# A two-stream GRU's last eight steps: r and z in one product, another order of turns, other places for late shares

## The chip, the cores and the metric

The kernel runs on one core of a Trainium2 chip. The metric is device time in microseconds (us) of one execution; lower is better. Each kernel is executed several times, and one further execution is recorded by the hardware profiler.

## The reference

Two layers work on x (64 sequences, 128 steps, 512 features, float32), with cond (64 x 512).

```python
x = x + L0(x, cond)      # gated linear recurrence, computed with cumulative sums
x = x + L1(cond, x)      # a conditioned GRU

# L1: 128 steps, one after the other, on h (64 x 512), h0 = 0
z  = sigmoid(x_t @ W_z + h @ U_z + vz)
r  = sigmoid(x_t @ W_r + h @ U_r + vr)
hh = tanh(x_t @ W + (r * h) @ U + vh)
h  = (1 - z) * h + z * hh
```

vz, vr and vh are products of cond with C_z, C_r, C, plus biases. The output is x after both residual sums, all 128 steps.

## The kernel before, in words

The first layer is done by feature chunks and takes the first third of the time. The rest of the span is the GRU, whose 128 steps depend on each other.

The 64 sequences are split into two streams of 32 (class Stream, s = 0 and 1). While one stream's step waits for its sigmoids and products, TensorE works for the other. A stream's state h is kept in a packed form: 128 partitions, of which each quarter of 32 holds the 32 sequences for 128 of the 512 features. hT is the same state transposed within 32 x 32 blocks, which makes it fit to be loaded as weights; U is the moving operand. matmuls (L459) takes a product apart in 4 parts of the contraction (k) and 4 quarters of the output (q); in float32 each of these 16 matmuls shows as two weight loads and two matmuls in the trace.

What does not depend on h, x_t @ W plus the v terms, is called a share. The shares of eight steps (a group) are computed together, as seven outer products of a fast (Strassen-Winograd) scheme with seven inner ones each (class Outer, products at L602, adds at L704 and L719 to L724). They are stored to DRAM (L732), read back for each stream and step as four transfers of 48 KB (load_share, L854 to L865), and copied into the PSUM tile g by ScalarE (put_share), where the products with h are then added up. Even steps are loaded into the tile xz (two buffers, one for each stream in effect), odd steps into the stream's whole_v. A load must therefore wait for the copy of the step two before it.

halves (L893) writes one step of one stream in two halves. In the ordinary order (steps up to 120) they are:

- first half: one product of 256 columns for r and z (of_state, L917); sigmoid r (L918); in two halves of the columns, r*h (L922) and its transposition (L923), both on DVE; sigmoid z (L927); on POOL 1-z (L933) and (1-z)*h (L934), both in the place of r. In the gaps go products of the next group (place), reads of finished ones, and the outputs of the step before (deferred).
- second half: the candidate product (L954, printed under L464), tanh (L957), the copy of the next share (L871), z*hh (L969), the new h (L970), its transposition (L974), and on POOL the sum with x for the output (L985).

From step 121 on (APART) no products of shares are left, and the halves become three parts: r's product of 128 columns; then z's product into a PSUM tile of its own (gz); then the candidate. A round, one step of both streams, takes the parts in the order 0 0 1 0 1 1. There ScalarE computes 1-z as sigmoid(-z) (L930), DVE computes (1-z)*h (L931) and the output's sum (L978), and the new h is made in two halves of the columns (L969 to L972), so that its first half can be loaded while the second is made. Outputs of the last eight steps are gathered in o_last and stored by L1028: four steps at once after step 123, two after steps 125 and 127.

Each engine runs its own queue in order. pin() keeps an instruction behind the one before it on its engine, as the program is written. The SP queue (SyncE) issues nearly all transfers; those that are not pinned may be put ahead by the scheduler at build time, by what it takes to be ready first.

Of the kernel before, what the change touches and what calls it, by code (L numbers as in the profile page):

```python
# [9 lines left out]
F32 = mybir.dt.float32  # L10
# [9 lines left out]
def kernel(  # L20
# [58 lines left out]
    def pin(instruction):  # L79
        return tc.keep_in_program_order(instruction)  # L80
# [751 lines left out]
    def direct(st, t):  # L832

        return t < 8

    class Stream:
        def __init__(self, s):
            self.s = s
            self.whole_v = vs[s]
            self.batches = slice(s * SB, (s + 1) * SB)  # L840
            self.h = self.hT = None

            self.g = psum.tile([P, 3, P], F32, tag="p0", name=f"g{s}")

            self.rz = fs[s][:, : 4 * P].rearrange("p (n e) -> p n e", e=P)
            self.home = self.g
            self.early = {}
            self.shares = {}  # L850
            self.outputs = {}
            self.gz = None

        def load_share(self, t):  # L854

            assert all((t, q) in stored for q in range(Q)), (self.s, t)
            if t % 2 == 0:
                share = work.tile([P, 3 * P], F32, tag="xz", bufs=2, name=f"xz{self.s}_{t}")
            else:
                share = self.whole_v.rearrange("p g e -> p (g e)")  # L860
            self.shares[t] = share
            n = t % TW * B + self.s * SB
            rows = shares_d[t // TW % len(shares_d)][n : n + SB]
            for q in range(Q):
                nc.sync.dma_start(share[q * SB : (q + 1) * SB], rows[:, q])  # L865

        def put_share(self, t):

            share = self.shares.pop(t).rearrange("p (g e) -> p g e", e=P)
            if t < APART:  # L870
                pin(nc.scalar.copy(self.g, share))  # L871
                return
            if self.gz is None:
                self.gz = psum.tile([P, 1, P], F32, tag="p2", name=f"gz{self.s}")
            pin(nc.scalar.copy(self.g[:, ::2], share[:, ::2]))
            pin(nc.scalar.copy(self.gz, share[:, 1:2]))

        def put_v(self):

# [13 lines left out]
        def halves(self, t, filler=None, between=None, targets=lambda: (0, 0), busy=False, reads=(4, 0)):  # L893
# [2 lines left out]

            r, z, rh, rhT = (self.rz[:, n] for n in range(4))
            h_, hT_, g = self.h, self.hT, self.g
            apart = t >= APART

            def of_state(gates, xT_, g=g):
                matmuls(
                    g if g is self.gz else g[:, gates],
                    lambda k: xT_[:, k * SB : (k + 1) * SB],
                    [w_s[:, k, gates] for k in range(K)],
                    start=False,
                )
# [6 lines left out]
            if t == 0:  # L914
                pin(nc.scalar.activation(z, g[:, 1], AF.Sigmoid))
            else:
                of_state(slice(0, 2 - apart), hT_)  # L917
                pin(nc.scalar.activation(r, g[:, 0], AF.Sigmoid))  # L918

                for n in range(2 - apart):  # L920
                    e = slice(0, P) if apart else slice(n * HC * SB, (n + 1) * HC * SB)
                    pin(nc.vector.tensor_tensor(rh[:, e], r[:, e], h_[:, e], ALU.mult))  # L922
                    pin(nc.vector.transpose(rhT[:, e], rh[:, e]))  # L923
                if apart:
                    yield
                    of_state(slice(1, 2), hT_, self.gz)
                pin(nc.scalar.activation(z, self.gz[:, 0] if apart else g[:, 1], AF.Sigmoid))  # L927

                if apart:
                    pin(nc.scalar.activation(r, self.gz[:, 0], AF.Sigmoid, scale=-1.0))  # L930
                    pin(nc.vector.tensor_tensor(r, r, h_, ALU.mult))  # L931
                else:
                    pin(nc.gpsimd.tensor_scalar(r, z, -1.0, 1.0, ALU.mult, ALU.add))  # L933
                    pin(nc.gpsimd.tensor_tensor(r, r, h_, ALU.mult))  # L934
            while shared_to_copy:
                shared_to_copy[0]()
            add(1)
# [24 lines left out]
            elif t == S - 1:  # L962
# [4 lines left out]
            for n in range(1 + apart) if t else ():  # L967
                e = slice(n * HC * SB, (n + 1) * HC * SB) if apart else slice(0, P)
                pin(nc.vector.tensor_tensor(hh[:, e], hh[:, e], z[:, e], ALU.mult))  # L969
                pin(nc.vector.tensor_tensor(h[:, e], hh[:, e], r[:, e], ALU.add))  # L970
                if apart:
                    pin(nc.vector.transpose(hT[:, e], h[:, e]))  # L972
            if not apart or t == 0:
                pin(nc.vector.transpose(hT, h))  # L974
            self.h, self.hT = h, hT

            def output():
                pin(nc.vector.tensor_tensor(o, o, h, ALU.add))  # L978
                self.store(t)

            if apart:
                deferred.append(output)
                return
            pin(
                nc.gpsimd.tensor_tensor(  # L985
# [9 lines left out]
                self.store(t)  # L995

            deferred.append(output)
            if APART <= t + AHEAD < S:
# [5 lines left out]
            if t + 2 < S and not direct(self, t + 2) and all((t + 2, q) in stored for q in range(Q)):  # L1004
                self.load_share(t + 2)

        def output(self, t):
            if t // 4 not in self.outputs:
# [10 lines left out]
        def store(self, t):  # L1019
            if t == S - 1 or t == S - 3:  # L1020
                ts = slice(t - 1, t + 1)
            elif t % 4 == 3:
                ts = slice(t - 3, t + 1)
            else:
                return
            for q in range(Q):
                queue = nc.scalar if t == S - 1 and self.s and q % 2 else nc.sync
                queue.dma_start(  # L1028
                    out_parts[q, self.batches, ts],
                    self.outputs[t // 4][q * SB : (q + 1) * SB, ts.start % 4 : (ts.stop - 1) % 4 + 1],  # L1030
                )

    APART, AHEAD = 121, 10
    last_outputs = []
    deferred = []
    pending = []
# [222 lines left out]
    def take(n):  # L1261
        st, ts = streams[order[n][0]], order[n][1]
        at = FIRST + n
        twice = n + 1 < len(order) and order[n + 1][0] == st.s
        busy = at < GOALS[3][0]
        todo = pending[:]
        pending.clear()
        together = min(order[n][1], order[min(n + 1, len(order) - 1)][1]) >= APART
        yield from st.halves(
            ts,  # L1270
            filler=lambda: [f() for f in todo],
            targets=lambda: (
                0 if together else goal(at + 1) - 1 - 2 * twice if busy else state["placed"] + 2,
                goal(at + 1 + st.s * together) + 2 * twice,
            ),
            busy=busy,
            between=lambda: late(n),
            reads=(0, 2) if together else (2, 2) if twice else (4, 1 * busy),
        )
        if ts + 1 in st.early:  # L1280
            st.g = st.early.pop(ts + 1)
        elif direct(st, ts + 1):
            st.put_v()
            f = lambda: st.x_products(ts + 1)
            f() if twice else pending.append(f)
        if n > 0 and order[n - 1][0] == st.s:
            return

        tick = 2 * order[n - st.s][1] + st.s if n else FIRST
        if tick in (FIRST, FIRST + 1):  # L1290
            sums_to_take.extend(sum_tasks(1)[tick - FIRST])
            take_sums(4)
        for w in range(2, NX):
            n_ = tick - 16 * w
            if w == 2 and n_ == -23:
                load_window(w)
                ahead_of[w] = gathers(w)
            elif w > 2 and -30 <= n_ < -26:
                load_window(w, qs=range(n_ + 30, n_ + 31))
                ahead_of[w] = gathers(w)  # L1300
            elif (-25 if w > 2 else -22) <= n_ < -21:
                gather(ahead_of[w], 2 if w > 2 else 4)
            elif w == 2 and n_ in (-20, -19):
                gather(ahead_of[w], 2)
            if n_ == (-21 if w > 2 else -19):
                sums_to_take.extend(sum_tasks(w))

    n = 0
    while n < len(order):
        together = n + 1 < len(order) and order[n][0] == 0 and order[n][1] >= APART  # L1310
        steps = [take(n + i) for i in range(1 + together)]

        for i in (0, 0, 1, 0, 1, 1) if together else (0, 0):
            next(steps[i], None)
        n += len(steps)
    while deferred:
# [36 lines left out]
```

## Time and profile before

| | us |
|---|---|
| median of 3 runs | 1877.04 |
| lowest and highest | 1876.59, 1879.87 |
| the profiled execution | 1878.12 |
| its span, first to last instruction | 1876.3 |
| TensorE busy | 1864.2 (99%) |
| VectorE (DVE) busy | 1504.9 (80%) |
| ScalarE (ACT) busy | 722.6 (39%) |
| GpSimd (POOL) busy | 865.1 (46%) |

The granted TensorE clock was 0.999 of full speed. All stamps below count from the start of the span. In rows of the timeline the columns are: start, duration, engine, line of the kernel, operation, output and inputs by the program's names ("fi" is the tile that holds r, z, r*h and its transposition; "h" the one that holds hh, the new h and hT), shapes, the number of instructions merged, and in brackets the idle time of the engine before it with what ended it. "issue" is idle time in which the profile shows nothing to wait for. In the windows table a row gives a stretch, its length, TensorE's busy time with the number of matmuls, the granted clock, the share of the DMA engines that was busy, and GB/s. The page's third part gives, for a DMA queue, packets, megabytes and share.

Step 120's first product starts at 1822.14; the first products of the rounds 121 to 127 start at 1830.06, 1835.31, 1841.71, 1847.39, 1853.79, 1859.52 and 1865.76.

### The profile page before, as it was taken

What the parts mean: (1) busy time and instruction counts of PE and PEld (TensorE: products, weight loads), DVE (VectorE), ACT (ScalarE), POOL (GpSimd) and SP (SyncE); (2) the same over time, 40 slices, a digit from 0 to 9 for tenths busy, and PEclk for the clock granted to TensorE, in tenths of its full rate; (3) what the DMA queues carried; (4) which work ended last, traced back from release to release, by engine and by line L of the source; (5) the groups of instructions that cost most, each with busy time, mean ns of one, the idle gap of its engine ahead of it and who ended that gap; (6) DMA issues with size and microseconds to landing.
All of it is one profiled execution on the core that took longest, in us unless ns stands there. A gap on an engine that the chain in (4) does not pass through costs nothing.

```text
span 1876.3 us, 62311 instructions
## 1 busy us (share of the span) xinstructions
PE 1864.2 (99%) x24793; PEld 1054.2 (56%) x24793; DVE 1504.9 (80%) x3438; ACT 722.6 (39%) x1888; POOL 865.1 (46%) x1544
## 2 busy tenths in 40 slices
PE   9999999999999999999999999999999999999998
PEld 5444444444444445566666666666666666666567
DVE  5899999999999976777777777777777777777786
ACT  3232223222232233344444444444444444444434
POOL 1233232333333344546556556466565565565650
PEclk9999999999999999999999999999999999999999
DMA  7765433444333241334334344344343343443343
GB/s 181 176 124 119 82 70 73 88 82 83 73 76 65 49 86 29 101 90 142 112 101 142 94 115 133 104 124 126 96 137 109 99 141 101 114 130 96 111 111 78
DMA packets 366754, 195.38 MB, mean 104 GB/s; under 512 B 225332, under 2 KB 352064, under 8 KB 366464
## 3 DMA queue, kind: packets, MB, share of 16 engines
q1 hardware_dynamic: 366280, 191.33, 40.9%
q8 instruction: 195, 3.19, 0.7%
q14 instruction: 95, 0.78, 0.1%
q10 hardware_dynamic: 184, 0.07, 0.0%
HBM read 78.63 MB, written 81.13 MB: 85 GB/s over the span
## 4 chain that ended last, share of the span: by engine, by line
PE 98%; DVE 1%; issue 0%; DMA 0%; ACT 0%; SPq 0%; DVEq 0%; ACTq 0%
PE g L464 36%; PE p L232 35%; PE r L602 14%; PE r12a L602 4%; PE shared L602 4%; PE r12b L602 4%; PE gz L464 1%; PE tp L190 0%; PE pv L464 0%; DMA x<-in_x_dram 0%; DVE W L704 0%; PE g_first L464 0%; DVE fi L923 0%; DVE fi L922 0%; DVE r L339 0%
## 5 line engine op out<-in xcount | busy, mean ns | idle before, releaser
L232 PE MATMUL p<-xT,W 128*128 128x512 f32 (+1 forms) x1560 | 661.9, 586 | 0.0
L232 PEld LDWEIGHTS p<-xT,W 128*128 128x128 f32 x1560 | 293.5, 190 | 361.6 <-issue 359.1
L464 PE MATMUL g<-w_s,h 128*32 128x256 f32 (+1 forms) x8128 | 481.0, 373 | 2.3 <-issue 1.6
L464 PEld LDWEIGHTS g<-w_s,h 128*32 128x32 f32 x8128 | 301.4, 110 | 179.4 <-issue 83.2
L464 PEld LDWEIGHTS g<-w_s,fi 128*32 128x32 f32 x8128 | 222.7, 109 | 113.9 <-issue 55.4
L464 PE MATMUL g<-w_s,fi 128*32 128x128 f32 x8128 | 276.3, 273 | 2.7 <-DVE fi L922 1.3
L922 DVE TENSOR_TENSOR fi<-fi,h 128x64 f32<-128x64 f32 (+1 forms) x494 | 112.3, 227 | 179.3 <-ACT fi L918 178.5
L985 POOL TENSOR_TENSOR h<-h,x 128x128 f32<-128x128 f32 x242 | 121.3, 501 | 232.4 <-DVE h L974 206.8
L314 POOL COPY first<-condT 128x4 f32<-128x4 f32 x64 | 12.6, 196 | 461.8 <-DVE h L386 432.8
L918 ACT ACTIVATE fi<-g 128x128 f32<-128x128 f32 x254 | 70.6, 278 | 327.7 <-PE g L464 308.9
L933 POOL TENSOR_SCALAR fi<-fi 128x128 f32<-128x128 f32 x240 | 72.6, 302 | 236.6 <-DVE fi L922 226.5
L704 DVE TENSOR_TENSOR W<-r,W 128x384 f32<-128x384 f32 x315 | 169.2, 539 | 7.4
L310 ACT ACTIVATE fi<-fi 128x512 f32<-128x512 f32 x64 | 40.4, 631 | 340.6 <-DVE fi L351 340.6
L957 ACT ACTIVATE h<-g 128x128 f32<-128x128 f32 x255 | 70.9, 278 | 236.2 <-PE g L464 236.2
L923 DVE STREAM_TRANSPOSE fi<-fi 128x64 f32<-128x64 f32 (+1 forms) x494 | 122.2, 247 | 22.8 <-PE r12a L602 0.5
L969 DVE TENSOR_TENSOR h<-h,fi 128x128 f32<-128x128 f32 (+1 forms) x264 | 94.9, 359 | 43.8 <-ACT h L957 43.1
L253 POOL TENSOR_TENSOR x<-xT,h 128x512 f32<-128x512 f32 x63 | 122.6, 1946 | 4.9
L934 POOL TENSOR_TENSOR fi<-fi,h 128x128 f32<-128x128 f32 x240 | 110.8, 462 | 20.0
L970 DVE TENSOR_TENSOR h<-h,fi 128x128 f32<-128x128 f32 (+1 forms) x264 | 97.7, 370 | 27.2 <-POOL held L810 0.9
L810 POOL TENSOR_TENSOR held<-held 128x128 f32<-128x128 f32 x240 | 113.7, 488 | 3.1
L602 PE MATMUL r<-w_inner,held 128*32 128x384 f32 x1080 | 114.6, 486 | 0.0
L339 DVE RECIPROCAL r<-r 128x256 f32<-128x256 f32 x60 | 104.2, 1737 | 0.0
(158 smaller groups left out, 2721.5 us busy)
## 6 DMA issues: line engine op xcount, KB each, us to landing
shares<-W SPq DMA_DIRECT2D x240, 192.0 KB, 2.1
xz<-shares SPq DMA_DIRECT2D x480, 48.0 KB, 1.9
whole_v<-shares SPq DMA_DIRECT2D x480, 48.0 KB, 2.0
x2d<-x SPq DMA_DIRECT2D x63, 256.0 KB, 4.2
words<-held SPq DMA_DIRECT2D x240, 64.0 KB, 2.1
out_dram<-o SPq DMA_DIRECT2D x240, 64.0 KB, 1.8
xw_None<-x2d SPq DMA_DIRECT2D x56, 256.0 KB, 3.4
w_rows<-in_L_cond_W_f_dram SPq DMA_DIRECT2D x4, 256.0 KB, 5.7
```

The costliest lines, as they stand in the source:

```text
L232: nc.tensor.matmul(p[:, tokens], lhsT=W0[:, c, n, k, :], rhs=xT[g][:, k, tokens], start=(k == 0), stop=(k == K - 1),)
L253: nc.gpsimd.tensor_tensor(x2.rearrange("p (t b) -> p t b", b=GB)[:, ts], xT[g][:, c, :].rearrange(f"{layout(g)} -> p t b", b=GB)[:, ts], b ...
L339: pin(nc.vector.reciprocal(r, r))
L464: nc.tensor.matmul(p[q * SB : (q + 1) * SB], lhsT=lhsT(k), rhs=part(wk, q), start=(start and k == 0), stop=(stop and k == len(w) - 1), ski ...
L602: nc.tensor.matmul(self.bank(bank)[q * SB : (q + 1) * SB], lhsT=a[:, q * SB : (q + 1) * SB], rhs=w_, start=start, stop=True, skip_group_ch ...
L704: pin(nc.vector.tensor_tensor(dst, r, other, ALU.add))
L810: pin(nc.gpsimd.tensor_tensor(*a))
L922: pin(nc.vector.tensor_tensor(rh[:, e], r[:, e], h_[:, e], ALU.mult))
L923: pin(nc.vector.transpose(rhT[:, e], rh[:, e]))
L934: pin(nc.gpsimd.tensor_tensor(r, r, h_, ALU.mult))
L970: pin(nc.vector.tensor_tensor(h[:, e], hh[:, e], r[:, e], ALU.add))
L985: nc.gpsimd.tensor_tensor(hh.rearrange("p (k b) -> p k b", b=SB), hT.rearrange("p (k b) -> p k b", b=SB), x_of(self, t), ALU.add,)
```

## The change

- The separate order now begins at step 120 (TURNS) instead of 121, and has two halves again: one product of 256 columns for r and z, and the candidate. A round's order is 0 1 0 1. The tile gz is gone; the share is copied to PSUM in one instruction.
- In these steps r*h is made and transposed in two halves; ScalarE still computes sigmoid(-z), into the place of r; (1-z)*h and the output's sum are on POOL.
- Shares of steps 123 to 127 (LATE) get places of their own, in v_x and held, whose contents are no longer needed. In the second half of step 120 a stream loads its shares up to step 125, in that of step 121 the rest. Share loads and output stores of steps from 120 on are pinned on their queue.

```diff
         def load_share(self, t):
-            if t % 2 == 0:
+            if t >= LATE:
+                share = late_shares(self.s, t)
+            elif t % 2 == 0:
                 share = work.tile([P, 3 * P], F32, tag="xz", bufs=2, name=f"xz{self.s}_{t}")
...
-                nc.sync.dma_start(share[q * SB : (q + 1) * SB], rows[:, q])
+                in_order(t, nc.sync.dma_start(share[q * SB : (q + 1) * SB], rows[:, q]))
...
         def put_share(self, t):
-            if t < APART:
-                pin(nc.scalar.copy(self.g, share))
-                return
...
-            pin(nc.scalar.copy(self.g[:, ::2], share[:, ::2]))
-            pin(nc.scalar.copy(self.gz, share[:, 1:2]))
+            pin(nc.scalar.copy(self.g, share))
...
-                of_state(slice(0, 2 - apart), hT_)
+                of_state(slice(0, 2), hT_)
                 pin(nc.scalar.activation(r, g[:, 0], AF.Sigmoid))
-                for n in range(2 - apart):
-                    e = slice(0, P) if apart else slice(n * HC * SB, (n + 1) * HC * SB)
+                for n in range(2):
+                    e = slice(n * HC * SB, (n + 1) * HC * SB)
                     pin(nc.vector.tensor_tensor(rh[:, e], r[:, e], h_[:, e], ALU.mult))
                     pin(nc.vector.transpose(rhT[:, e], rh[:, e]))
-                if apart:
-                    yield
-                    of_state(slice(1, 2), hT_, self.gz)
-                pin(nc.scalar.activation(z, self.gz[:, 0] if apart else g[:, 1], AF.Sigmoid))
-                if apart:
-                    pin(nc.scalar.activation(r, self.gz[:, 0], AF.Sigmoid, scale=-1.0))
-                    pin(nc.vector.tensor_tensor(r, r, h_, ALU.mult))
+                pin(nc.scalar.activation(z, g[:, 1], AF.Sigmoid))
+                if turns:
+                    pin(nc.scalar.activation(r, g[:, 1], AF.Sigmoid, scale=-1.0))
                 else:
                     pin(nc.gpsimd.tensor_scalar(r, z, -1.0, 1.0, ALU.mult, ALU.add))
-                    pin(nc.gpsimd.tensor_tensor(r, r, h_, ALU.mult))
+                pin(nc.gpsimd.tensor_tensor(r, r, h_, ALU.mult))
...
             def output():
-                pin(nc.vector.tensor_tensor(o, o, h, ALU.add))
+                pin(nc.gpsimd.tensor_tensor(o, o, h, ALU.add))
                 self.store(t)
+            def load_next(last):
+                for n in range(t + 2, min(last, S - 1) + 1):
+                    if n not in self.shares and not direct(self, n) and all((n, q) in stored for q in range(Q)):
+                        self.load_share(n)
-            if apart:
+            if turns:
                 deferred.append(output)
+                load_next(max(t + 2, S - 1 if t > TURNS else LATE + 2))
                 return
...
-    APART, AHEAD = 121, 10
+    TURNS, AHEAD, LATE = 120, 10, 123
+    def in_order(t, transfer):
+        return pin(transfer) if t >= TURNS else transfer
+    def late_shares(s, t):
+        n = 2 * (t - LATE) + s
+        if n < Q:
+            return v_x[:, n].rearrange("p g e -> p (g e)")
+        return held.rearrange("p n e -> p (n e)")[:, (n - Q) * 3 * P : (n - Q + 1) * 3 * P]
...
-        for i in (0, 0, 1, 0, 1, 1) if together else (0, 0):
+        for i in (0, 1, 0, 1) if together else (0, 0):
             next(steps[i], None)
```

More of the change, by code (lines that the diff above doesn't have):

```diff
@@ L851, in __init__ @@
             self.outputs = {}
-            self.gz = None
         def load_share(self, t):
             assert all((t, q) in stored for q in range(Q)), (self.s, t)
-            if t % 2 == 0:
+            if t >= LATE:
+                share = late_shares(self.s, t)
+            elif t % 2 == 0:
                 share = work.tile([P, 3 * P], F32, tag="xz", bufs=2, name=f"xz{self.s}_{t}")
@@ L864, in load_share @@
             for q in range(Q):
-                nc.sync.dma_start(share[q * SB : (q + 1) * SB], rows[:, q])
+                in_order(t, nc.sync.dma_start(share[q * SB : (q + 1) * SB], rows[:, q]))
         def put_share(self, t):
             share = self.shares.pop(t).rearrange("p (g e) -> p g e", e=P)
-            if t < APART:
-                pin(nc.scalar.copy(self.g, share))
-                return
-            if self.gz is None:
-                self.gz = psum.tile([P, 1, P], F32, tag="p2", name=f"gz{self.s}")
-            pin(nc.scalar.copy(self.g[:, ::2], share[:, ::2]))
-            pin(nc.scalar.copy(self.gz, share[:, 1:2]))
+            pin(nc.scalar.copy(self.g, share))
         def put_v(self):
@@ L898, in halves, with of_state @@
             h_, hT_, g = self.h, self.hT, self.g
-            apart = t >= APART
-            def of_state(gates, xT_, g=g):
+            turns = t >= TURNS
+            def of_state(gates, xT_):
                 matmuls(
-                    g if g is self.gz else g[:, gates],
+                    g[:, gates],
                     lambda k: xT_[:, k * SB : (k + 1) * SB],
@@ L966, in halves @@
                 return
-            for n in range(1 + apart) if t else ():
-                e = slice(n * HC * SB, (n + 1) * HC * SB) if apart else slice(0, P)
+            for n in range(1 + turns) if t else ():
+                e = slice(n * HC * SB, (n + 1) * HC * SB) if turns else slice(0, P)
                 pin(nc.vector.tensor_tensor(hh[:, e], hh[:, e], z[:, e], ALU.mult))
                 pin(nc.vector.tensor_tensor(h[:, e], hh[:, e], r[:, e], ALU.add))
-                if apart:
+                if turns:
                     pin(nc.vector.transpose(hT[:, e], h[:, e]))
-            if not apart or t == 0:
+            if not turns:
                 pin(nc.vector.transpose(hT, h))
@@ L977, in output @@
             def output():
-                pin(nc.vector.tensor_tensor(o, o, h, ALU.add))
+                pin(nc.gpsimd.tensor_tensor(o, o, h, ALU.add))
                 self.store(t)
-            if apart:
+            def load_next(last):
+                for n in range(t + 2, min(last, S - 1) + 1):
+                    if n not in self.shares and not direct(self, n) and all((n, q) in stored for q in range(Q)):
+                        self.load_share(n)
+            if turns:
                 deferred.append(output)
+                load_next(max(t + 2, S - 1 if t > TURNS else LATE + 2))
                 return
@@ L997, in halves @@
             deferred.append(output)
-            if APART <= t + AHEAD < S:
+            if TURNS <= t + AHEAD < S:
                 pin(nc.gpsimd.tensor_copy(ident.rearrange("p (k b) -> p k b", b=SB), x_of(self, t + AHEAD)))
@@ L1003, in halves @@
             read(reads[1])
-            if t + 2 < S and not direct(self, t + 2) and all((t + 2, q) in stored for q in range(Q)):
-                self.load_share(t + 2)
+            load_next(t + 2)
         def output(self, t):
@@ L1027, in store @@
                 queue = nc.scalar if t == S - 1 and self.s and q % 2 else nc.sync
-                queue.dma_start(
-                    out_parts[q, self.batches, ts],
-                    self.outputs[t // 4][q * SB : (q + 1) * SB, ts.start % 4 : (ts.stop - 1) % 4 + 1],
-                )
-    APART, AHEAD = 121, 10
+                in_order(
+                    t,
+                    queue.dma_start(
+                        out_parts[q, self.batches, ts],
+                        self.outputs[t // 4][q * SB : (q + 1) * SB, ts.start % 4 : (ts.stop - 1) % 4 + 1],
+                    ),
+                )
+    TURNS, AHEAD, LATE = 120, 10, 123
[6 more added lines that the diff above has]
+        return held.rearrange("p n e -> p (n e)")[:, (n - Q) * 3 * P : (n - Q + 1) * 3 * P]
     last_outputs = []
@@ L1267, in take @@
         pending.clear()
-        together = min(order[n][1], order[min(n + 1, len(order) - 1)][1]) >= APART
+        together = min(order[n][1], order[min(n + 1, len(order) - 1)][1]) >= TURNS
         yield from st.halves(
@@ L1273, in take @@
                 0 if together else goal(at + 1) - 1 - 2 * twice if busy else state["placed"] + 2,
-                goal(at + 1 + st.s * together) + 2 * twice,
+                goal(at + 1) + 2 * twice,
             ),
@@ L1277, in take @@
             between=lambda: late(n),
-            reads=(0, 2) if together else (2, 2) if twice else (4, 1 * busy),
+            reads=(2, 0) if together else (2, 2) if twice else (4, 1 * busy),
         )
@@ L1309 @@
     while n < len(order):
-        together = n + 1 < len(order) and order[n][0] == 0 and order[n][1] >= APART
+        together = n + 1 < len(order) and order[n][0] == 0 and order[n][1] >= TURNS
         steps = [take(n + i) for i in range(1 + together)]
-        for i in (0, 0, 1, 0, 1, 1) if together else (0, 0):
+        for i in (0, 1, 0, 1) if together else (0, 0):
             next(steps[i], None)
```

## The prediction

> **What bounds the kernel now.** I read the page first, then the last steps in the windows table, then single rows of the timeline.
>
> ```profile
> q8 instruction: 195, 3.19, 0.7%
> ...
> PE 98%; DVE 1%; issue 0%; DMA 0%; ACT 0%; SPq 0%; DVEq 0%; ACTq 0%
> ```
>
> The chain that ended last is TensorE for 98% of the span, so up to step 119, where the diff changes no arithmetic, nothing can be gained. All that matters lies in the last 54 us (1822.14, the first r,z product of step 120, to 1876.3). There each pair of steps (one of each stream: a round) has 3.49 us of r,z products (2 x 32 instructions of 256 columns, 1.73 each, or the same work in 128 columns) and 1.75 us of candidate products (2 x 0.873): 5.24 us. The windows run from one round's first product to the next, for steps 120, 122 and 123:
>
> ```profile
> 1822.14:1830.06 7.92, 5.65 (x136) 1.00 0.54 143
> ...
> 1835.31:1841.71 6.40, 5.74 (x197) 1.00 0.36 83
> 1841.71:1847.39 5.68, 5.55 (x203) 1.00 0.31 74
> ```
>
> The six rounds of steps 121 to 126 run from 1830.06 to 1865.76: 5.95 us each, 0.71 above the products. Step 120, still in the ordinary order, takes 7.92. Part of the 0.71 is not a wait for data:
>
> ```profile
> 1836.33 0.75 PE L464 MATMUL g<-w_s,h 128*32 128x128 f32 x19 [0.42 <-issue]
> ...
> 1840.27 0.75 PE L464 MATMUL gz<-w_s,h 128*32 128x128 f32 x20 [0.24 <-issue]
> ```
>
> TensorE stops with nothing to wait for, and between the two stops lie 127 recorded matmuls and as many weight loads, about 254 instructions in 3.94 us. The page's instruction queue moved 195 packets in the kernel for 49,586 TensorE instructions, 254 for each. So late rounds, which need 6 x 64 = 384 instructions in 5.24 us, outrun the instruction supply: 384/254 x 3.94 = 5.96 us, the measured round.
>
> **The change, part by part.**
>
> *One r,z product of 256 columns.* It removes 64 matmuls and 64 weight loads a round (256 instructions are left, worth 3.97 us at the supply's pace). The supply stops binding; what is next late is the dependency chain.
>
> *The new chain of a round.* Stream 1's step 120 already shows the r,z form with halves of the transposition:
>
> ```profile
> 1826.18 1.91 PE L464 MATMUL g<-w_s,h 128*32 128x256 f32 x32
> ...
> 1828.16 0.28 ACT L918 ACTIVATE fi<-g 128x128 f32<-128x128 f32 x1 [0.84 <-PE g L464]
> ...
> 1828.97 0.18 DVE L922 TENSOR_TENSOR fi<-fi,h 128x64 f32<-128x64 f32 x1
> ...
> 1829.19 0.43 PE L464 MATMUL g<-w_s,fi 128*32 128x128 f32 x8 [1.10 <-DVE fi L922]
> ...
> 1829.31 0.30 POOL L933 TENSOR_SCALAR fi<-fi 128x128 f32<-128x128 f32 x1 [0.94 <-DVE fi L922]
> ```
>
> From the start of an r,z product to its candidate product are 3.01 us. The way back to the next r,z product is in step 123:
>
> ```profile
> 1844.77 1.11 PE L464 MATMUL g<-w_s,fi 128*32 128x128 f32 x32
> ...
> 1845.93 0.28 ACT L957 ACTIVATE h<-g 128x128 f32<-128x128 f32 x1 [0.60 <-PE g L464]
> ...
> 1846.76 0.25 DVE L972 STREAM_TRANSPOSE h<-h 128x64 f32<-128x64 f32 x1
> ```
>
> Candidate start to first transposed half is 1.99 us; a transposition releases TensorE 0.39 after its start (1828.80 to 1829.19): 2.38. In the new order stream 0's candidate starts when stream 1's r,z product has gone by (3.46 after stream 0's, later than 3.01, so no stall), and the next round starts 2.38 later: 1.73 + 1.73 + 2.38 = 5.84 us. That is the floor, 0.11 under today's round.
>
> *A wait that is added.* ScalarE's sigmoid of -z writes the place of r, which the second half of r*h still reads. POOL's L933 above has that very wait today: it starts 0.16 after L922's end at 1829.15. Today's late rounds don't have it, since their r*h is long done. For stream 1 the sigmoid now starts 3.07 to 3.13 after its r,z product; queued behind it on ScalarE is stream 0's tanh, which would be due at 1.73 + 1.16 = 2.89 and now starts 0.17 after it, at 3.24 or later. DVE and the next round's first product wait for that tanh: +0.35, a round of 6.19.
>
> *r*h of (1-z) and the output's add go from DVE to POOL* (three or four adds and products of 0.46 us a round). POOL is otherwise empty, so that hides; but not when it meets DVE:
>
> ```profile
> 1800.38 0.61 POOL L985 TENSOR_TENSOR h<-h,x 128x128 f32<-128x128 f32 x1 [2.26 <-DVE h L974]
> ...
> 1800.59 0.48 DVE L922 TENSOR_TENSOR fi<-fi,h 128x64 f32<-128x64 f32 x1
> ```
>
> This L922 took 0.48 where it takes 0.23 alone, and ended 0.08 after POOL. Stream 1's product on POOL runs from about 3.44 to 3.90 after its r,z product, and DVE's first multiply of stream 0's new state is due at 3.55: +0.25 if they meet, a round of 6.44. I take 6.3 between them; bounds 5.84 and 6.5. Six rounds: 6 x (6.3 - 5.95) = +2.1 us (-0.7 to +3.3).
>
> The Trainium skill's page "SBUF — State Buffer", section "SBUF: two separate sides", says that a DVE operation with two SBUF inputs and a GpSimd operation share one port pair under an exclusive lock, held for the whole instruction. It speaks against this part; the row of 0.48 agrees with it. By the rule every round pays the meeting, 6 x (6.44 - 5.95) = +2.9; were the lock absent, 6 x (6.19 - 5.95) = +1.4.
>
> *Step 120 joins the late order.* Its two stalls of 1.17 and 1.10 us go. Stream 1's state is transposed only at 1824.71, so its r,z product starts at 1824.78, 0.9 late; then +1.73 + 2.38 = 1828.89, with the added wait 1829.24. The step takes 7.1 instead of 7.92: -0.8 (-1.2 to -0.6).
>
> *Step 127.* Today r's product to the last tanh takes 1872.21 - 1865.76 = 6.45; new 1.73 + 3.01 + 1.16 = 5.90. Stream 1's candidate may also wait until ScalarE has read z from the same PSUM place (today's loads for a candidate show such a wait for L927); that would give back 0.4. I take -0.3 (-0.55 to -0.15).
>
> *The end.* Stream 0's four stores take SP 4 x 0.47 = 1.88 us. Today they are through 0.4 before stream 1's (the tanhs are 2.12 apart). In the new order the tanhs are 0.93 apart, so stream 1's two stores on SP queue for 0.95: +0.9 (0 to +1.0).
>
> *Late shares.* This is the dearest part. At step 120 the code now queues shares 122, 123, 124 and 125 of stream 0 and only then those of stream 1: 32 transfers, pinned in this order on SP, behind the store of the last block of shares.
>
> ```profile
> 1824.25 5.12 SPq L1028 DMA_DIRECT2D out_dram<-o  x8
> 1829.41 0.45 SPq L732 DMA_DIRECT2D shares<-W  x1
> ```
>
> SP issues one transfer in 0.47 us (1829.41, 1829.91, 1830.39). Today that store is at 1829.41 behind eight output stores, and stream 1's share 122 is complete right after it. In the new order stream 1's share 122 is the 17th to 20th transfer: if the first starts at 1829.9, the last starts 19 x 0.47 = 8.93 later, lands 1.9 later (page: 1.9 for such a share), 1840.75, and is copied to PSUM in 0.48: 1841.25. Its r,z product is due at 1822.14 + 7.1 + 6.3 + 1.73 = 1837.3. TensorE waits 4.0, and behind the copy on ScalarE wait stream 0's sigmoids of step 122, so nothing else can run. Later shares land in time (stream 1's 123 by 1842.6, wanted after 1844). Bounds: if SP reaches the loads as soon as the block's add is done (1826.2), the share is there at 1837.5 and costs 0.3 to 1.0; if stream 1's share 121, now pinned behind output stores, pushes everything by 1.3, up to 5.0, and one transfer of 1.69, as SP had in this stretch, adds 1.2. I take 4.0, nearest to today's SP rows. The places of their own cost nothing: v_x and held have no reader left by then (the last product from held ends at 1820.8).
>
> **Sum.** +2.1 - 0.8 - 0.3 + 0.9 + 4.0 = +5.9 us on the profiled run of 1878.12 us (its span of 1876.3 and 1.8 around it), which lies 1.1 above the median of 1877.04; against the median, 1882.9. Ends of the terms: -0.7 - 1.2 - 0.55 + 0 + 1.0 = -1.5, and 3.3 - 0.6 - 0.15 + 1.0 + 6.2 = +9.8.
>
> **Rivals.** 0.2% is 3.75 us, about what a measurement of this kernel can tell from no change.
>
> *The share is no bottleneck* (the loads get ahead of the output stores on SP). Without its 4.0 the sum is +1.9: 1878.9, no difference. For it: the add that the last store needs ends at 1826.1. Against: SP was in front of the adds with eight stores then.
>
> *The chain is shorter than the rows say, faster.* If tanh doesn't wait behind the sigmoid and halves overlap so that a round comes to 5.3, near the 5.24 of products, six rounds give -3.9, step 120 -1.2, step 127 -0.55: -5.6, 1871.4. It decides from a round below about 5.6 with stream 1's share 122 in PSUM by 1837. Against: the rows 3.01 and 2.38 are bare latencies with idle engines, and 5.84 follows from them.
>
> *The supply of instructions still binds:* 256 instructions against 254 a block, 0.24 to 0.42 a round, at most +2.5 more: 1885.4, inside the forecast's side. Against: the ordinary order ran 336 instructions in the 8.0 us from 1806.2 without such a stop, the pace of 256 in 6.1.
>
> **How the numbers follow.** Slower by more than 3.75 us: 0.66 (the queue of shares as reckoned, rounds no quicker than today's). Within: 0.29 (0.24 for a harmless queue, 0.05 for a queue that costs 1 to 2 us and short rounds). Faster: 0.05, the short chain. The range 1877.0 to 1887.0 takes in the upper end of the terms and most of the harmless case.
>
> **What would show it.** In the changed trace: "issue" stops on TensorE gone; rounds of steps 123 to 126 at 6.2 to 6.5 us; round 122 near 10 with ScalarE's copy of stream 1's share 122 waiting for a DMA; sigmoid of -z starting after L922; step 120 near 7.1. Wrong if round 122 is like the others, or if rounds are below 5.8.

## The result, and the profile after

The changed kernel takes 1887.99 us in the median (1887.2 to 1889.15, 6 runs) where the kernel before, run beside it, takes 1877.19: a ratio of 1.0054, interval 1.0044 to 1.0064, so 10.8 us slower. The profiled execution took 1888.15 us with a span of 1886.4; that is 10.0 above the profiled execution before (1878.12).

The page: the chain that ended last now has a share of SP's queue.

```profile
PE 97%; DVE 2%; SPq 1%; issue 0%; ACT 0%; DMA 0%; POOL 0%; DVEq 0%; ACTq 0%; POOLq 0%
```

The windows table, TensorE alone, from one round's first product to the next; the last two numbers of a row are the share of the DMA engines and GB/s, the one before them is the granted clock. Round 122 is cut in three:

```profile
1821.69:1829.22 7.53, 5.83 (x137) 1.00 0.45 125
1829.22:1835.87 6.65, 5.62 (x129) 1.00 0.47 126
1835.87:1842.09 6.22, 1.93 (x32) 0.83 0.40 103
1842.09:1845.51 3.42, 3.42 (x33) 0.50 0.39 104
1845.51:1848.60 3.09, 2.76 (x69) 0.79 0.28 63
1848.60:1855.23 6.63, 5.62 (x128) 1.00 0.34 88
```

The other rounds, 123 to 126, are alike within 0.01 us. Against the kernel before, span by span, the 10.1 us go as follows. Step 120's first product starts 0.45 earlier (over all traces of this case, whatever the edit, it starts between 1821.07 and 1822.38, so this need not come from the change). Step 120 takes 7.53 instead of 7.92: -0.39. Six rounds at 6.635 instead of 5.95: +4.1. Round 122 takes 12.73, 6.1 more than its neighbours. Step 127 to the last tanh takes 6.46 (before 6.45): 0. From that tanh to the end 4.80 instead of 4.09: +0.7. Sum: -0.45 - 0.39 + 4.1 + 6.1 + 0.7 = +10.1.

The timeline of SP shows why round 122 is long. "xz" are the shares of step 122, stream 0's and, 16 transfers later, stream 1's:

```profile
1829.68 0.43 SPq L732 DMA_DIRECT2D shares<-W  x1
1830.21 1.78 SPq L866 DMA_DIRECT2D xz<-shares  x4
1832.04 4.31 SPq L866 DMA_DIRECT2D W<-shares  x8
1836.45 1.76 SPq L866 DMA_DIRECT2D held<-shares  x4
1838.30 1.76 SPq L866 DMA_DIRECT2D xz<-shares  x4
```

And what TensorE and ScalarE do meanwhile (timeline of the same kernel):

```profile
1841.56 0.48 ACT L871 COPY g<-xz 128x384 f32<-128x384 f32 x1 [5.59 <-DMA xz<-shares]
...
1842.09 3.64 PE L464 MATMUL g<-w_s,h 128*32 128x256 f32 x32 [4.29 <-ACT g L871]
```

The wait ends with the copy. But the product that follows takes 3.42 us to the next one where it takes 1.73 elsewhere, at a granted clock of 0.50.

The end of a regular round, 124 (it starts at 1855.23), up to the next round's product:

```profile
1859.12 0.87 POOL L969 TENSOR_TENSOR o_last<-o_last,h 128x128 f32<-128x128 f32 x2
...
1859.32 0.34 DVE L917 TENSOR_TENSOR fi<-fi,h 128x64 f32<-128x64 f32 x1 [0.71 <-ACT fi L913]
...
1859.94 0.18 DVE L917 TENSOR_TENSOR fi<-fi,h 128x64 f32<-128x64 f32 x1
1860.21 0.28 ACT L922 ACTIVATE fi<-g 128x128 f32<-128x128 f32 x1 [0.76 <-DVE fi L917]
...
1860.39 0.27 ACT L948 ACTIVATE h<-g 128x128 f32<-128x128 f32 x1
...
1860.54 1.08 PE L464 MATMUL g<-w_s,fi 128*32 128x128 f32 x32 [0.78 <-ACT fi L922]
1860.57 0.46 POOL L925 TENSOR_TENSOR fi<-fi,h 128x128 f32<-128x128 f32 x1 [0.57 <-ACT fi L922]
...
1860.69 0.42 DVE L960 TENSOR_TENSOR h<-h,fi 128x64 f32<-128x64 f32 x1 [0.22 <-ACT h L948]
...
1861.87 0.42 PE L464 MATMUL g<-w_s,h 128*32 128x256 f32 x4 [0.24 <-DVE h L960]
```

Sigmoid(-z) (L922) waits for the second half of r*h (L917, 1859.94); tanh of stream 0 (L948), whose candidate was finished before, goes behind it, 5.16 us after the round's first product; and two multiplies on DVE, 0.34 and 0.42 us long instead of 0.23, meet instructions of POOL: the output's adds (L969) and (1-z)*h (L925). No stop for "issue" is left on TensorE's matmuls in these rounds.

### The profile page after: what moved, and what is told of

It is laid out like the page before. It is cut to its first block, busy times and chain, and to the rows that moved or that the text cites. A ratio compares the mean times of both kernels' runs of the same rounds, so it can differ in the third digit from the quotient of the medians.

```text
span 1886.4 us, 61458 instructions
## 1 busy us (share of the span) xinstructions
PE 1866.6 (99%) x24345; PEld 1046.8 (55%) x24345; DVE 1503.2 (80%) x3446; ACT 720.5 (38%) x1876; POOL 874.9 (46%) x1570
## 4 chain that ended last, share of the span: by engine, by line
PE 97%; DVE 2%; SPq 1%; issue 0%; ACT 0%; DMA 0%; POOL 0%; DVEq 0%; ACTq 0%; POOLq 0%
PE g L464 36%; PE p L232 35%; PE r L602 14%; PE r12a L602 4%; PE shared L602 4%; PE r12b L602 4%; PE tp L190 1%; SPq L866 0%; PE pv L464 0%; DVE W L704 0%; DVE fi L917 0%; DVE fi L918 0%; DVE h L960 0%; PE g_first L464 0%; PE idle L139 0%
## 5 line engine op out<-in xcount | busy, mean ns | idle before, releaser
L464 PE MATMUL g<-w_s,h 128*32 128x256 f32 x8128 | 490.7, 380 | 7.1 <-ACT g L871 4.3
L917 DVE TENSOR_TENSOR fi<-fi,h 128x64 f32<-128x64 f32 x508 | 114.5, 225 | 191.3 <-ACT fi L913 190.5
L948 ACT ACTIVATE h<-g 128x128 f32<-128x128 f32 x255 | 70.7, 277 | 229.5 <-PE g L464 229.5
L925 POOL TENSOR_TENSOR fi<-fi,h 128x128 f32<-128x128 f32 x254 | 117.0, 460 | 62.8 <-ACT fi L922 42.9
L918 DVE STREAM_TRANSPOSE fi<-fi 128x64 f32<-128x64 f32 x508 | 124.7, 245 | 24.3 <-PE r12a L602 0.5
```

The costliest lines, as they stand in the source:

```text
L464: nc.tensor.matmul(p[q * SB : (q + 1) * SB], lhsT=lhsT(k), rhs=part(wk, q), start=(start and k == 0), stop=(stop and k == len(w) - 1), ski ...
```

## The experiments

Each kernel was timed beside the kernel before on one chip. The median of before moved between jobs from 1877.3 to 1878.5, so the ratios are the firmer numbers. The expectations reckon from some 1877 to 1877.5 for the kernel before; from "Order and place together" on it ran at 1877.9 to 1878.5, so up to 1 us of a miss in the plain times is due to that.

**Shares in the order of use.** In the changed kernel:

```diff
-                load_next(max(t + 2, S - 1 if t > TURNS else LATE + 2))
+                load_next({TURNS: t + 2, TURNS + 1: t + 3, TURNS + 2: t + 4}.get(t, S - 1))
```

> The changed kernel, but the late shares are queued in the order of use: at step 120 each stream loads only its share 122, at 121 its shares 123 and 124, at 122 those of 125 and 126, at 123 that of 127. Theory (the place in SP's queue makes stream 1's share 122 late; the wait of 4.3 us and the half clock after it, 1.7 to 1.8 us, follow from that): round 122 falls from 12.73 to 6.63 us and the kernel to 1888.0 - 6.1 = 1881.9. Rival (the share is late whatever its place, because its transfers or the rows they read are late): round 122 stays above 10 us, 1887 to 1888.

1882.09 us, ratio 1.0025 (1.0015 to 1.0036). Round 122 runs from 1835.75 to 1842.40, 6.65 us, as long as a regular round, and the product after the copy is at full clock. So the place in SP's queue, not the transfers, made the share late, and the order of 16 transfers cost 5.4 (by the ratios) to 5.9 us (by the medians). A smaller wait is left in round 123 (7.06).

**The clock.** Needless products fill the wait:

```diff
+            if (self.s, t) == (1, TURNS + 2):
+                hT0 = streams[0].hT
+                for gates in (slice(0, 2), slice(0, 2), slice(2, 3)):
+                    matmuls(banks["s"][:, gates], lambda k: hT0[:, k * SB : (k + 1) * SB],
+                            [w_s[:, k, gates] for k in range(K)])
```

> The changed kernel with 4.3 us of needless products (stream 0's state with U, into a PSUM tile that nobody reads) on TensorE in the wait of round 122; nothing else differs. Theory (the r,z product after the wait takes 3.42 instead of 1.73 us because the clock was halved after some 2 us of idle time): the product takes 1.73 us at granted clock 1.0, round 122 is 1.6 us shorter, 1886.4. Rival (that product waits for something else, as its instructions or ScalarE): it still takes 3.4 us, 1888.0.

In the total nothing is seen: 1888.37 us, 1.0060 (1.0045 to 1.0075). In the rows it is: the needless products run from 1837.34, and the product after the wait,

```profile
1842.96 1.93 PE L464 MATMUL g<-w_s,h 128*32 128x256 f32 x32 [1.08 <-ACT g L871]
```

takes 1.75 us to the next at granted clock 1.00, and round 122 is 12.22 us long instead of 12.73 (1835.62 to 1847.84). From the start of the share's copy to round 123 it is 5.42 us (1842.42 to 1847.84) instead of 7.04 (1841.56 to 1848.60): 1.62 less, as expected. But the copy itself started 6.80 us after the round's first product, not 5.69, since SP took longer for the transfers before it and for its own in this run. Why was not settled, so the total neither confirms nor denies; the clock as the cause of the slow product rests on the rows.

**A place of its own for sigmoid(-z):**

```diff
+                    r = held[:, 4, (2 + self.s) * P : (3 + self.s) * P]
                     pin(nc.scalar.activation(r, g[:, 1], AF.Sigmoid, scale=-1.0))
```

> The changed kernel, but sigmoid(-z) goes to a place of its own (the last 256 columns of held), so that it doesn't wait for r*h to read r. Theory (this wait holds tanh of stream 0 on ScalarE, and the candidate of stream 1, which writes the PSUM place that the sigmoid reads): a round falls from 6.63 to 6.0 to 6.2 us, the idle time before stream 1's candidate from 0.78 to about 0.4, the kernel by some 3 to 4.5 us to 1883.5 to 1885. Rival (rounds are long since POOL and DVE meet, whatever ScalarE does): rounds stay above 6.5, 1887 to 1888.

Rounds of 6.22 us (1849.27 to 1855.49, and so on), 0.41 less. Tanh of stream 0 now waits for its own candidate alone,

```profile
1860.08 0.28 ACT L949 ACTIVATE h<-g 128x128 f32<-128x128 f32 x1 [0.20 <-PE g L464]
```

and starts 4.59 us after the round's first product (1855.49) instead of 5.16, so the wait for r's place is real. A part of this 0.57 is lost again: (1-z)*h on POOL comes earlier too, and now meets the second half of r*h, which takes 0.42 us. The idle time before stream 1's candidate falls from 0.78 to 0.28. But the total gains 1.2 only (1886.8; 1.0051, 1.0036 to 1.0066; by the ratios 0.6): the share of step 122 comes when it comes, and TensorE waits longer for it:

```profile
1842.56 3.64 PE L464 MATMUL g<-w_s,h 128*32 128x256 f32 x32 [5.52 <-ACT g L871]
```

**Adds on DVE again:** (1-z)*h and the output's add.

```diff
-                pin(nc.gpsimd.tensor_tensor(r, r, h_, ALU.mult))
+                pin((nc.vector if turns else nc.gpsimd).tensor_tensor(r, r, h_, ALU.mult))
...
-                pin(nc.gpsimd.tensor_tensor(o, o, h, ALU.add))
+                pin(nc.vector.tensor_tensor(o, o, h, ALU.add))
```

> The changed kernel, but (1-z)*h and the output's add of the late steps are on DVE, as in the kernel before. Theory (stream 0's first multiply of the new state, 0.42 us, and stream 1's first half of r*h, 0.35 us, are lengthened by POOL's operations; without POOL they take 0.23): 0.1 to 0.3 us less a round, 1886 to 1887.3; all of it is not won, since (1-z)*h now stands on DVE ahead of that multiply. Rival (those durations have nothing to do with POOL): they stay at 0.42 and 0.35, and the round grows by the 0.29 of the operation on DVE, 1889 to 1890.

Rounds of 6.23 us (1854.96 to 1861.19), 0.40 less, more than the 0.1 to 0.3 expected. The two multiplies are short again:

```profile
1858.99 0.23 DVE L917 TENSOR_TENSOR fi<-fi,h 128x64 f32<-128x64 f32 x1
...
1860.29 0.22 DVE L960 TENSOR_TENSOR h<-h,fi 128x64 f32<-128x64 f32 x1
```

A multiply lengthened by 0.12 at the head of the chain delays sigmoid(-z), and with it tanh: here tanh starts 4.98 us after the round's first product, 0.18 sooner, and from tanh to the next round it is 1.25 us instead of 1.48. Here too the late share takes most of the gain: 1886.86 (1.0051, 1.0034 to 1.0068).

**Order and place together.** The two edits above.

> The changed kernel with the shares in the order of use and with a place of its own for sigmoid(-z). Theory (the two losses are independent; the own place brings rounds of 6.22 us where the others had 6.64): seven rounds of 0.42 below 1882.1, that is 1879.1, with no round over 6.4. Rival (the late shares only move on to another step when rounds get shorter): a round with a wait for a DMA remains, 1880 to 1882.

1880.46 us, 1.0012 (1.0002 to 1.0021). Rounds 124 to 126 are 6.22, as the theory had it, but 121 to 123 take 7.13, 6.56 and 6.47, with waits for shares, as the rival had it; the time lies in the rival's range.

**All three.**

> As before it, and (1-z)*h and the output's add on DVE too. Theory (the wait for r's place and the meetings of POOL and DVE are two separate lengths of the chain of a round, 0.42 and 0.40 by the runs so far): rounds of 5.84 us, the floor of bare latencies, 1876.4. Rival (they shorten the same stretch, or (1-z)*h now stands ahead of stream 0's first multiply on DVE): rounds of 6.1 to 6.2, 1878.5 to 1879.

1879.54 us, 1.0008 (0.9999 to 1.0018). Rounds from 123 on take 6.11, as the rival had it: the place and the meetings are partly the same stretch (0.41 and 0.40 alone, 0.52 together), and (1-z)*h now stands ahead of DVE's first multiply. In the profiled execution, which was the slowest of the ten (1881.67 us), rounds 121 and 122 take 7.42 and 7.81:

```profile
1836.68 5.35 PE L464 MATMUL g<-w_s,h 128*32 128x256 f32 x64 [1.53 <-ACT g L871]
```

Even stream 0's share 122 is now late, by 1.53 us, at the end of round 121: its loads are pinned behind the last store of shares (1830.67 here, 1829.68 in the changed kernel). In round 122 TensorE waits for no share, but these 64 matmuls take 5.35 us where they take 3.66 elsewhere. In the windows table,

```profile
1837.00:1840.00 3.00, 3.00 (x36) 0.50 0.40 100
```

the granted clock is 0.50: after a wait of 1.53 us it was the clock that cost round 122 its 1.7 us.

**The kernel before from step 120.** One part of the change alone: APART = 120 in the kernel before, and reads=(2, 0) for those steps.

> The kernel before with one part of the change alone: its late order of six products begins at step 120 instead of 121 (and the last waiting block is read in the second part of step 120). Theory (step 120 loses its two stalls of 1.17 and 1.10 us but stream 1's state of step 119 is still 0.9 late, and one more round goes at the pace of the instruction supply): step 120 takes 6.6 to 7.1 instead of 7.92 us, 1876.0 to 1876.5. Rival (the stalls come back as a wait for stream 1): 7.9, 1877.3.

1879.57 us in the median (1876.76 to 1881.82), 1.0008 (0.9998 to 1.0017). Step 120 takes 6.21 us in the profiled execution, but the six rounds after it average 6.22 instead of 5.95, with stops for "issue" up to 0.55 and a wait of 0.61 for a share's copy. What step 120 gains is given back; neither expectation had that. In the kernel before, the first round of the late order, 121, runs without a stop (5.25 us, 1830.06 to 1835.31); here step 120 is the first, and round 121 has stops already (6.52, 1827.72 to 1834.24).

**A wider product in the kernel before.**

```diff
-                of_state(slice(0, 2 - apart), hT_)
+                of_state(slice(0, 2 - (apart and self.s == 1)), hT_)
```

> The kernel before, but stream 0's product for r in the late steps has 256 columns (the second half goes to a part of g that nobody reads): the same number of instructions, 0.87 us more of product time in each of seven rounds. Theory (the late rounds of the kernel before go at the pace of the instruction supply, 5.95 us for 384 instructions, and the products fill only 5.24 of it): the added time falls into the stops, rounds of 6.1 to 6.2, +1 to +2 us: 1878.3 to 1879.3. Rival (the stops come from the data or from the products themselves): all of it shows, 7 x 0.87 = +6.1, 1883.4.

1878.98 us, 1.0006 (0.9997 to 1.0015): 6.1 us of product time were added and some 1.1 show. The rounds are 6.09 us, all product (6.11), without a stop (starts of stream 0's products for r, 122 and 123):

```profile
1836.41 1.94 PE L464 MATMUL g<-w_s,h 128*32 128x256 f32 x32
...
1842.50 1.94 PE L464 MATMUL g<-w_s,h 128*32 128x256 f32 x32
```

In the kernel before, rounds 122 to 126 average 6.09 too (1835.31 to 1865.76): there the added 0.87 fell wholly into the stops, and what shows is mostly round 121, which had none (5.25, now 6.09). So from round 122 on the kernel before does go at the pace at which TensorE gets its instructions.

**What the runs point to, in the changed kernel.** The three edits, loads of step 122 not pinned (in_order from LATE on), and stream 1's (1-z)*h in its second half, behind stream 0's new state.

> The changed kernel with what the runs so far point to: shares in the order of use, those of step 122 no longer pinned (so that they can be issued before the last store of shares, as in the kernel before), sigmoid(-z) in its own place, the adds on DVE, and stream 1's (1-z)*h only in its second half, behind stream 0's new state on DVE. Theory (rounds 121 and 122 of the run with all three lost 1.3 and 1.7 us to shares that came late, and a round of 6.11 still had 0.27 of (1-z)*h ahead of stream 0's multiply): all rounds 5.84 to 5.9, about 1874.5 to 1875.5, faster than the kernel before by 2 to 3 us. Rival (the shares of step 122 are late since SP is full with stores until 1829.5, pinned or not): rounds 121 and 122 together still above 13 us, 1877 to 1879.

1876.70 us, 0.9991 (0.9982 to 1.0000). Six times the same round (121 to 126), no wait for a share; the first two:

```profile
1828.40:1834.31 5.91, 5.61 (x129) 1.00 0.49 127
1834.31:1840.22 5.91, 5.62 (x128) 1.00 0.36 87
```

That is 11 us below the changed kernel, with the same products in the same order. By the ratio it is 1.7 us below the kernel before, where 2 to 3 were expected: a round is 5.91, not 5.84, and from the last tanh to the end it is still 4.8 us, as in the changed kernel. The last two edits were not run apart.

**A mixed order in the kernel before.** Stream 0 has one product of 256 columns, stream 1 keeps two:

```diff
+            split = apart and self.s == 1
...
-                of_state(slice(0, 2 - apart), hT_)
+                of_state(slice(0, 2 - split), hT_)
...
+                if split:
+                    of_state(slice(1, 2), hT_, self.gz)
...
+                    if not split:
+                        r = held[:, 4, 3 * P :]
```

> The kernel before, but in its late steps (from 121) stream 0 has one product of 256 columns for r and z, with r*h in halves and sigmoid(-z) in a place of its own; stream 1 keeps its products of 128 columns, and the order stays r,z of 0; r of 1; candidate of 0; z of 1; candidate of 1. Theory (the supply needs 320 instead of 384 instructions a round, 4.96 us; the products 5.24; stream 0's candidate can't start before 3.01 after its r,z product, 0.41 later than TensorE is free): rounds of 5.6 to 5.7 instead of 5.95, 6 x 0.3 = 1.8 us, 1875.5 to 1876. Rival (shares, which have one buffer less time in shorter rounds, come late): some round waits for a DMA, no gain, 1877 to 1878.

1876.96 us, 0.9994 (0.9985 to 1.0003). The rounds are 5.64, as worked out, without a stop for "issue", and the last one waits for stream 1's share 127, as the rival had it:

```profile
1867.58 1.08 PE L464 MATMUL g<-w_s,h 128*32 128x128 f32 x32 [2.08 <-ACT g L875]
```

**The same from step 120** (APART = 120):

> The same from step 120. Theory: step 120 takes some 6.2 instead of 7.92 us as in the run of the kernel before from 120, 1.5 us less again, 1874 to 1874.5. Rival (that run gave its gain back because loads and stores on SP fall behind): the gain of step 120 is lost again by step 127, 1876 to 1879.

1876.52 us, 0.9990 (0.9982 to 0.9999): step 120 takes 6.21, rounds 5.64, and the wait of 2.00 us in round 127 stays. The time lies in the rival's range.

**With the changed kernel's places for late shares.** The mixed order from step 120, with late_shares, in_order from step 123 on, and the order of use.

> The last one (kernel before from step 120, stream 0 with one product of 256 columns), with the changed kernel's late places for the shares of 123 to 127, loaded in the order of use and pinned from step 123 on. Theory (that run lost 2.0 us of TensorE's time to stream 1's share 127, which could be loaded only when its single buffer was free and SP had issued the stores of steps 124 and 125): no wait for a share is left, all rounds 5.64 to 5.7, 2.0 us less: 0.2% below the kernel before at the least, 1874 to 1875 where that is 1877 to 1878. Rival (the stores, now pinned behind more loads, end the kernel later): the rounds are short, but what follows the last tanh grows from 4.2 to 5 or 6 us, 1876 to 1877.

1873.90 us (1873.5 to 1875.57) beside 1877.85: 0.9979 (0.9970 to 0.9988), faster than both kernels. Every round from 121 on is 5.64 and step 127 has no wait:

```profile
1855.77 2.82 PE L464 MATMUL g<-w_s,h 128*32 128x256 f32 x64
...
1861.42 2.81 PE L464 MATMUL g<-w_s,h 128*32 128x256 f32 x64
```

From the last tanh to the end it is 4.5 us (4.3 in the run before it), so the rival did not come. Here the change's third part, the places for late shares and their pinned loads, removes the wait of 2.00 us; by the ratios the two runs differ by 2.1 us, by the medians by 2.6. Shorter rounds need shares sooner than a single buffer can give them.

## Why the prediction was wrong, point by point

The direction held, and so did the mechanisms that the prediction named; the time, 1887.99, is 1.0 above the range. Two steps failed: the six rounds were put at 6.3 us and took 6.635, since POOL and DVE meet twice a round and not at most once (+2.0 us); and the late share was priced by its wait alone, with nothing for the half clock after it (+2.1, of which 0.3 is a longer wait). Against the sum of +5.9, the profiled executions differ by +10.1: 2.0 and 2.1 from these two, 0.4 from step 120, 0.3 from step 127, less 0.2 at the end and the 0.45 by which step 120 started earlier.

- *The kernel before goes at the pace of its instruction supply in the late rounds.* Right for rounds 122 to 126; the wider product shows it (6.1 us added, 1.1 seen), and the stops are gone after. That the reckoned 5.96 met the mean of 5.95 so closely is luck: the mean holds round 121, 5.25 us without a stop, and five rounds of 6.09.
- *The floor of a round in the new order is 5.84 us.* Right, nearly: 5.91 when all else was cleared away. With a place of its own for sigmoid(-z) tanh came 4.59 us after the round's first product, where the working has 1.73 + 2.89 = 4.62.
- *Six rounds at 6.3, at most 6.5.* Wrong in size: 6.635, +4.1 us instead of +2.1. Both causes were named, the wait for r's place and the meeting of POOL and DVE at the new state's multiply. What the working lacked is POOL's two output adds, which meet the first half of stream 1's r*h (0.34 us). This multiply stands at the head of the chain, so sigmoid(-z) came 3.25 us after stream 1's product and tanh 3.43, not 3.1 and 3.24. With the adds on DVE they came after 3.08 and 3.25, and the round was 6.23, where the working had 6.19 without a meeting. So the mis-sized step is the meetings: they cost 0.40 us a round, where 6.3 held 0.11 for them, and 6.44 one whole meeting of 0.25. There are two.
- *Stream 1's share 122 is late by 4.0 us.* The wait was 4.29, and the reason, 16 transfers of stream 0 ahead of it, is shown by the order of use. That 4.0 came so near is in part luck: the share was in PSUM at 1842.04, not 1841.25, but TensorE was also free for it later, at 1837.80, not 1837.3. What was missed altogether is what TensorE's clock does in such a wait: 1.7 us more for the next product. The term was 6.1, not 4.0.
- *Step 120 gains 0.8.* It gained 0.39, outside the stated bounds. The working had counted the wait for r's place here, but no meeting; the new state's multiply takes 0.42 us in this step too (1828.04), beside POOL's L925, and with the adds on DVE the step took 7.29 instead of 7.53.
- *Step 127 gains 0.3.* It gained nothing; stream 1's candidate waits 0.78 for sigmoid(-z) to leave its PSUM place, which the prediction had put at 0.4.
- *The end loses 0.9.* It lost 0.7: a term sized a little too high, within its bounds.
- The Trainium skill's page "SBUF — State Buffer", section "SBUF: two separate sides", has a DVE instruction with two SBUF inputs and a GpSimd instruction that reads SBUF exclude each other for an instruction's length. The rows agree that one waits for the other: 0.42 and 0.34 us beside POOL's instructions, 0.22 and 0.23 with these moved away. They don't show that the later one begins only after the other's end: the multiply of 0.42 ends 0.08 us after POOL's L925 (1861.11 and 1861.03), though it takes 0.22 alone. The working applied the rule to one POOL instruction of a round; the output's adds make a second.

Of the rivals, the harmless queue is refuted by the wait of 4.29, the short chain (5.3 us a round) by rounds of 6.635, and of 5.91 at the least, and the supply by the absence of stops.

## What to carry to other kernels

When a late transfer is moved in a queue, count every transfer that now stands ahead of the one needed first, and add what an idle engine costs afterwards, not the wait alone. A faster stretch ahead of a wait for a fixed arrival gains nothing: two edits that each saved 0.4 us a round gained only some 1 us in the total, and the first of them 2.4 once the shares were in order (ratios of 1.0025 and 1.0012). And before merging instructions to spare an engine, find out which limit comes next: here merging for one stream of two was enough to free the supply, and left the shorter chain (rounds of 5.64 us, not 5.91).

## What the runs showed of the hardware

The granted clock of TensorE fell to half within a wait of 4.3 us. TensorE is idle from 1837.8; in the windows table of the changed kernel,

```profile
1838.50:1839.50 1.00, 0.00 (x0) 1.00 0.49 118
...
1839.50:1840.50 1.00, 0.00 (x0) 0.73 0.37 102
...
1846.00:1847.00 1.00, 1.00 (x28) 0.61 0.06 9
```

a mean of 0.73 puts the fall to 0.5 at about 1840.0, after 2.2 us, and a mean of 0.61 the return at about 1846.8, 4.7 us after work began again at 1842.09. Other traces of this case differ. The fall came 4.4 us into the wait of 5.52 (own place) and 4.5 us into that of 5.57 (adds on DVE). In the run with all three a wait of 1.53 us was enough: the clock fell 0.2 us after work had begun again. The waits of 2.08 and 2.00 us in round 127 of the two mixed orders left it at 1.00, as did those of 0.8 in every round. What is alike is how long the half clock lasted, by windows of 0.05 to 0.1 us: 6.83 us here (1839.96 to 1846.79), 6.83 with the own place (1841.47 to 1848.30), 6.83 with the adds on DVE (1841.07 to 1847.90) and 3.41 with all three (1836.90 to 1840.31), that is twice 3.41 or once. The page "TensorE: Matmul & The Clock Gate" of the Trainium skill, section "What's actually happening", gives about 3.4 us for both changes, in windows that run on whatever the kernel does. The lengths agree with that; the idle time before a fall, 1.5 to 4.5 us, is not one figure here.

In rounds 122 to 126 of the kernel before, an instruction stream of some 64 instructions a microsecond was as much as TensorE was given: 254 in 3.94 us between two stops. Round 121 ran ahead of that, 384 in 5.25 us. What limits the stream was not tested.
